# Joint stages between scans: one fixed order of beats, convolution on four engines, gate on GpSimd, input norm folded into in_proj, rows backwards last

## The chip, the core and the metric

The kernel runs on one core of one Trainium2 chip. The metric is the device time of one execution in microseconds (us). The core's engines are named as in the profile: PE (matrix products; PEld loads its weights), DVE (VectorE), ACT (ScalarE), POOL (GpSimd) and SP, whose queue issues the DMAs.

## What is computed

The input is four images of 64 x 64 positions with 96 channels. Two layers of a selective-scan block are followed by two layers of linear attention and a quantised feed-forward net on the 4096 positions of each image as tokens. Layers 0 and 1 are, cut to what matters (`_gn` is a group norm over 32 groups of 3 channels, without weights):

```python
x = x + block(_gn(x))                      # twice, with each layer's weights
# block:
xz = jnp.einsum('bhwc,ec->bhwe', x, in_proj_w)          # 96 -> 384 channels
xp, z = jnp.split(xz, 2, axis=-1)
xc = conv3x3_per_channel(xp) + conv_b                   # 192 channels, 'SAME'
xc = jax.nn.silu(xc)
# four directions: rows, columns, rows backwards, columns backwards
ys = _selective_scan(xs, delta, A, Bmat, Cmat, Dp)      # h = exp(dl*A)*h + dl*u*B; y = C.h + D*u
y = ys[:, 0] + flip(ys[:, 2]) + wh_back(ys[:, 1]) + wh_back(flip(ys[:, 3]))
y = _layernorm(y, out_norm_w, out_norm_b)               # over 192 channels
y = y * jax.nn.silu(z)
return jnp.einsum('bhwd,cd->bhwc', y, out_proj_w)       # 192 -> 96 channels
```

## The kernel before

The four images go in two pairs, and a pair in one layer is a unit of work: layer 0 pair 0, layer 0 pair 1, layer 1 pair 0, layer 1 pair 1. The 2 x 192 inner channels of a pair fill three tiles of 128 partitions, `u0` and `u1` with 128 channels of one image each and `u2` with the last 64 of both. For each unit `hybrid_kernel` (L940) calls `between_scans` (L142) and then the scan, `PairScan.run` (L483). After the fourth scan `token_layers` (L889) does the rest.

A *scan* has 48 steps (4 directions `k` x 4 chunks of 1024 positions x 3 tiles) of 8 groups each. All its instructions on PE, DVE, ACT and POOL keep the order of the program through `InOrder` (L56). The sum over the state is transposed on PE, copied by ACT to the tile `ysum` (L661 to L665) and stored to `y` in device memory; directions after the first load the sum so far (`kept`, L653) and add to it. The directions come in the order 0 to 3, and in directions 2 and 3 the chunks go from the last to the first (`chunk_of`, L385); 1 and 3 run along columns. `begin` (L394) makes the first projections and the first step size (`xps`, `delta`, `du`, `dut`) of a scan and is called from the joint stage before it. Each step multiplies `h` by `cb` on POOL as its last work.

A *joint stage* (`between_scans`) is made of two generators, and the first stage has only the first of them. `scan_inputs` (L157) prepares the unit to come: it loads `wi`, makes nine diagonal matrices `diag` from the convolution weights on POOL (L172), clears the edges of three padded images `img`, and then `project` (L216) takes one image's 512 positions at a time: load x, normalise it on DVE with mean and 1/deviation of the group norm (`xn`, L223), three products on PE (`ips`, L227), two copies by ACT into `img` (L229, L230) and two silus to `zs`, stored to `zg` (L233 to L236). There are 16 such calls. The convolution is cut into pieces of 8 or 16 rows of one tile. `conv_product` (L183) does 8 rows on PE, nine taps as products of the shifted image with `diag` (`cps`, L189; each product appears as two records), then a silu on ACT (L190). `conv_chain` (L194) does 16 rows on DVE: one TENSOR_SCALAR (L203) and eight SCALAR_TENSOR_TENSOR (L205, "a tap" below), then a silu (L206). PE has eight pieces, DVE eight of double length. For layer 0, whose group norm has not been measured by an earlier unit, `measure` (L208) loads each image once more for its statistics, in the first joint stage only.

`scan_outputs` (L272) finishes the unit whose scan has just ended, in 16 groups of 256 positions from the first row on: load `zt`, `xr` and `ys` (L285 to L296), statistics of the layer norm on DVE (`ystats` L303, `ymv` L304, `ln_ve` L79), the power -1/2 on POOL (`ln_rs`, L81), `shift` on DVE (L307), normalise on ACT (L311), transposes on PE (`pt`, L319), four evictions with weight and bias on ACT (`gt`, L321), the gate `gt*zt` on DVE (L328), the out-projection on PE (`po`, L335), the residual sum on DVE (`xo`, L337) with its store, and two statistics for the next layer's group norm (`GroupNorm.take`, L117). At the end two chains of small operations (`GroupNorm.norm`, L120) give the next layer's mean and 1/deviation, one for each image.

Within a joint stage the order of each engine's instructions is decided by a scheduler, which starts from the order in which the generators' pieces are called. The stage's tiles come from pools of its own, whose memory is shared with the scan's pools; in the profile `wo`, the first tile to be loaded, is issued after the last store of `ysum`. PSUM has five buffers for inputs (`mm`), two for `pt` and one for `po`.

The scan's long-lived pool `s_q` holds, with one buffer each, the tiles `delta`, `du`, `dut` and the parts of the projection for even chunks.

Of the kernel before, what the change touches and what calls it, by code (L numbers as in the profile page):

```python
# [18 lines left out]
NB = 4  # L26
# [8 lines left out]
K = 4  # L35
NP = 32 * 3
# [7 lines left out]

# [5 lines left out]

# [4 lines left out]

class InOrder:  # L56

# [5 lines left out]

# [11 lines left out]

# [8 lines left out]

class ScanLayer:

# [21 lines left out]

class GroupNorm:


    def __init__(self, pool, pn, name, parts):
        self.pool, self.pn, self.name, self.n = pool, pn, name, 0
        self.stats = pool.tile([C, parts, 6], F32, name=f"{name}_stats", bufs=1)

    def take(self, nc, v):
        nc.vector.bn_stats(self.stats[:, self.n], v)  # L117
        self.n += 1

    def norm(self, nc, pp, tag, cst, half):  # L120
        pool = self.pool
        mv = pool.tile([C, 2], F32, name="mv")
        nc.vector.bn_aggr(mv, self.stats.rearrange("c g s -> c (g s)"))

        gm = pp.tile([C, 1], F32, name="gm", tag=tag)
        nc.tensor.matmul(gm, cst["group"], mv[:, 0:1], start=True, stop=True)
        mean = pool.tile([C, 1], F32, name="mean")
        nc.vector.tensor_copy(mean, gm)
        dev = pool.tile([C, 1], F32, name="dev")
        nc.vector.tensor_tensor(dev, mv[:, 0:1], mean, ALU.subtract)  # L130
        spread = pool.tile([C, 1], F32, name="spread")
        nc.vector.scalar_tensor_tensor(spread, dev, dev, mv[:, 1:2], ALU.mult, ALU.add)
        gv = pp.tile([C, 1], F32, name="gv", tag=tag)
        nc.tensor.matmul(gv, cst["group"], spread, start=True, stop=True)
        rs = rstd_of(nc, pool, gv, [C, 1], "gn", half[:C, 0:1])
        kept = self.pn.tile([C, 2], F32, name=f"{self.name}_norm")
        nc.vector.tensor_copy(kept[:, 0:1], mean)
        nc.vector.tensor_copy(kept[:, 1:2], rs)
        return kept[:, 0:1], kept[:, 1:2]


def between_scans(tc, cst, ident, half, pn, u, before, scan, after):  # L142


    with ExitStack() as stage:
        ins = scan_inputs(tc, stage, cst, ident, half, pn, u, scan, *after)
        if before is not None:
            pp = stage.enter_context(tc.tile_pool(name="c_ps", bufs=2, space=PSUM))
            outs = scan_outputs(tc, stage, cst, ident, half, pn, *before, pp)
            for g, _ in enumerate(outs):  # L150
                for _ in range(2 if g % 4 == 3 else 1):
                    next(ins, None)
        for _ in ins:
            pass


def scan_inputs(tc, stage, cst, ident, half, pn, u, scan, layer, pr):  # L157

    nc = tc.nc
    par, zg, x_src = layer.par, layer.zg[pr], layer.x_src
    pa = stage.enter_context(tc.tile_pool(name="a", bufs=1))
    p2 = stage.enter_context(tc.tile_pool(name="a2", bufs=3))
    pp = stage.enter_context(tc.tile_pool(name="a_ps", bufs=5, space=PSUM))

    wi = pa.tile([C, 2, 2 * DI], F32, name="wi")
    nc.sync.dma_start(out=wi, in_=layer.w["wi"].rearrange("i c d -> c i d"))

    diag = pa.tile([128, 9, 128], F32, name="diag")  # L170
    for tap in range(9):
        nc.gpsimd.tensor_scalar(diag[:, tap], ident, par[:, 0, P_CONV + tap : P_CONV + tap + 1], None, ALU.mult)  # L172

    imgs = []
    for j in range(3):
        img = pa.tile([128, HW + 2, HW + 2], F32, name=f"img{j}", tag=f"img{j}")
# [4 lines left out]
        imgs.append(img)  # L181

    def conv_product(j, c):  # L183

        ps = pp.tile([128, 8, HW], F32, name="cps", tag="mm")
        for tap in range(9):
            dy, dx = divmod(tap, 3)
            v = imgs[j][:, c + dy : c + dy + 8, dx : dx + HW]
            nc.tensor.matmul(ps, diag[:, tap], v, start=(tap == 0), stop=(tap == 8))  # L189
        nc.scalar.activation(  # L190
            u[j][:, HW * c : HW * (c + 8)], ps.rearrange("p h w -> p (h w)"), AF.Silu, bias=par[:, 0, P_CB : P_CB + 1]
        )

    def conv_chain(j, c):  # L194

        s, cols = j // 2, slice(HW * c, HW * (c + 16))
        to = u[j][:, cols].rearrange("p (h w) -> p h w", w=HW)
        for tap in range(9):
            dy, dx = divmod(tap, 3)
            v = imgs[j][:, c + dy : c + dy + 16, dx : dx + HW]  # L200
            weight = par[:, s, P_CONV + tap : P_CONV + tap + 1]
            if tap == 0:
                nc.vector.tensor_scalar(to, v, weight, par[:, s, P_CB : P_CB + 1], ALU.mult, ALU.add)  # L203
            else:
                nc.vector.scalar_tensor_tensor(to, v, weight, to, ALU.mult, ALU.add)  # L205
        nc.scalar.activation(u[j][:, cols], u[j][:, cols], AF.Silu)  # L206

    def measure(b):  # L208
        norm = GroupNorm(p2, pn, f"gn{b}", 8)
        for g in range(8):  # L210
            xt = p2.tile([C, 512], F32, name="xt", bufs=4)
# [882 lines left out]
```

## Time and profile before

| what | us |
|---|---|
| median of three runs | 10594.62 (10580.44 to 10601.88) |
| span of the profiled execution | 10592.1 |
| joint stage 0 (inputs alone) | 156.4 |
| joint stages 1, 2, 3 (outputs and inputs) | 205.6, 209.1, 202.4 |
| four scans | 2293 to 2298 each |
| token stage, with the last outputs | 635.8 |

The stages can be told apart in the trace by the scan operations on DVE: a joint stage lies between the last TENSOR_TENSOR_SCAN of one unit and the first of the next. The lines of the profile are read as follows. A line of a group has the line of the code, engine, operation, output <- inputs, shapes, and then the busy time in us, the mean duration of one in ns, and the idle time ahead of it with what ended it. A line of a wait has the engine with the waiting line, what it waited for, the total in us, how often and the longest. A line of the timeline has the start and the duration in us.

The whole of the profiled execution keeps DVE busy for 9610.8 us, POOL for 9023.9, ACT for 8761.4 and PE for 8027.2.

### The profile page before, as it was taken

What the parts mean: (1) busy time and instruction counts of PE and PEld (TensorE: products, weight loads), DVE (VectorE), ACT (ScalarE), POOL (GpSimd) and SP (SyncE); (2) the same over time, 40 slices, a digit from 0 to 9 for tenths busy, and PEclk for the clock granted to TensorE, in tenths of its full rate; (3) what the DMA queues carried; (4) which work ended last, traced back from release to release, by engine and by line L of the source; (5) the groups of instructions that cost most, each with busy time, mean ns of one, the idle gap of its engine ahead of it and who ended that gap; (6) DMA issues with size and microseconds to landing.
All of it is one profiled execution on the core that took longest, in us unless ns stands there. A gap on an engine that the chain in (4) does not pass through costs nothing. (4 is left out here: it accounts for less than half of the span.)

```text
span 10592.1 us, 142441 instructions
## 1 busy us (share of the span) xinstructions
PE 8027.2 (76%) x47648; PEld 5946.6 (56%) x47648; DVE 9610.8 (91%) x6922; ACT 8761.4 (83%) x18779; POOL 9023.9 (85%) x5298
## 2 busy tenths in 40 slices
PE   7777777777777777777877777777877777777666
PEld 4555555554555555555555555555555565555554
DVE  8999999998999999998899999999799999999755
ACT  6888888885988888887788888888688888888666
POOL 3999999993999999997599999999399999999645
PEclk9888898989888898998888988898888989899877
DMA  5677777776677777777567777777667777777710
GB/s 155 208 212 216 220 220 218 219 218 164 205 212 212 218 220 218 217 220 210 158 206 213 219 220 220 223 213 216 162 207 212 216 213 225 221 217 213 195 32 25
DMA packets 905174, 2120.41 MB, mean 200 GB/s; under 512 B 330582, under 2 KB 640152, under 8 KB 706712
## 3 DMA queue, kind: packets, MB, share of 16 engines
q1 hardware_dynamic: 904440, 2111.30, 69.5%
q8 instruction: 378, 6.19, 0.3%
q14 instruction: 356, 2.92, 0.1%
HBM read 1949.56 MB, written 161.48 MB: 199 GB/s over the span
## 5 line engine op out<-in xcount | busy, mean ns | idle before, releaser
L71 POOL TENSOR_TENSOR h<-h,cb 128x1024 f32<-128x1024 f32 x3072 | 7196.5, 2367 | 226.4 <-issue 62.6
L71 DVE TENSOR_TENSOR_SCAN h<-da,last,bp 128x1024 f32<-128x1024 f32 x2064 | 4736.6, 2335 | 146.7 <-PE bp L71 22.8
L71 ACT ACTIVATE x<-dut,bt 128x128 f32<-128x128 f32 x12288 | 3495.9, 371 | 1.4 <-PE bp L71 1.1
L71 PE MATMUL yp<-ident,h 128*128 128x128 f32 x24576 | 3359.4, 297 | 10.5 <-POOL h L71 10.5
L71 PEld LDWEIGHTS yp<-ident,h 128*128 128x128 f32 x24576 | 3188.5, 157 | 126.6 <-issue 76.6
L71 ACT ACTIVATE da<-delta,amat 128x1024 f32<-128x1024 f32 x2752 | 3062.3, 1139 | 96.6 <-DVE h L71 95.8
L71 PE MATMUL bp<-ident,x 128*128 128x128 f32 x10240 | 1678.5, 316 | 1294.1 <-DVE h L71 956.8
L71 PEld LDWEIGHTS bp<-ident,x 128*128 128x128 f32 x10240 | 1361.3, 163 | 1854.8 <-ACT x L71 1017.4
L71 DVE TENSOR_TENSOR bp<-du,bp 128x1024 f32<-128x1024 f32 x1472 | 1780.5, 1214 | 259.8 <-PE bp L71 257.8
L71 DVE TENSOR_TENSOR_SCAN h<-da,bp 128x1024 f32<-128x1024 f32 x688 | 1537.7, 2275 | 49.9 <-ACT da L71 9.6
L71 PE MATMUL bp<-bparts,sel 96*128 96x512 bf16 x2944 | 920.5, 398 | 756.3 <-DVE h L71 740.4
L71 PEld LDWEIGHTS <-sel 96*128 96x128 bf16 x2944 | 226.8, 100 | 1550.2 <-DVE h L71 1037.8
L71 ACT ACTIVATE bp<-delta,amat 128x1024 f32<-128x1024 f32 x320 | 358.1, 1119 | 526.3 <-DVE h L71 524.6
L71 POOL TENSOR_TENSOR dbu<-du,bb 128x1024 f32<-128x1024 f32 x320 | 755.7, 2362 | 0.0
L71 DVE TENSOR_TENSOR_SCAN h<-bp,last,dbu 128x1024 f32<-128x1024 f32 x240 | 558.9, 2329 | 16.9 <-POOL dbu L71 15.9
L71 PE MATMUL xps<-u,wx 128*76 128x512 f32 x720 | 532.2, 824 | 0.0
L71 POOL COPY last<-h 128x2 f32<-128x2 f32 x1152 | 217.7, 189 | 357.2 <-DVE h L71 355.5
L81 POOL TENSOR_TENSOR ln_rs<-ln_ve,half 128x4 f32<-128x4 f32 x64 | 89.8, 1403 | 483.1 <-DVE ln_ve L79 405.9
L71 ACT ACT_TABLE_LOAD x380 | 487.5, 1283 | 15.9 <-PE bp L71 9.2
L71 POOL TENSOR_TENSOR du<-delta,u 128x1024 f32<-128x1024 f32 x188 | 496.8, 2642 | 0.0
L71 PE MATMUL dps<-cdt,wdt 12*128 12x512 f32 x752 | 433.6, 656 | 0.0
L71 ACT COPY ysum<-yp 128x1024 f32<-128x1024 f32 x192 | 194.5, 1013 | 287.1 <-PE yp L71 287.1
(159 smaller groups left out, 6312.6 us busy)
## 6 DMA issues: line engine op xcount, KB each, us to landing
cb<-crow SPq DMA_DIRECT2D x1024, 1024.0 KB
cb<-crow SPq DMA_DIRECT2D x1024, 512.0 KB
bb<-crow SPq DMA_DIRECT2D x384, 256.0 KB
bb<-crow SPq DMA_DIRECT2D x128, 512.0 KB
y<-ysum SPq DMA_DIRECT2D x192, 256.0 KB
kept<-y SPq DMA_DIRECT2D x160, 256.0 KB
y<-ysum SPq DMA_DIRECT2D x64, 512.0 KB
zt<-zg SPq DMA_DIRECT2D x64, 384.0 KB
```

The lines of the kernel that those rows point to most:

```text
L71: return self.tc.keep_in_program_order(getattr(self.engine, op)(*args, **kwargs))
L81: nc.gpsimd.tensor_tensor(rs, ve, half, ALU.pow)
```

## The change

The joint stage becomes two classes, `Inputs` and `Outputs`, whose methods are called in one written order of 16 beats and a lead beat of -1. All four compute engines keep that order through `InOrder`; SP's DMAs don't. In beat b POOL gates group b-1; ACT normalises group b; DVE takes the statistics of group b+1, POOL its `ln_rs` and `shift` (two small POOL operations, where it was one on DVE); up to three image pieces are projected; group b is transposed; group b-1 is projected out and stored. Six times in a beat `fill` hands out convolution taps to three kinds of piece: 5 taps a beat to DVE, 3 products to PE, 3 taps to the new third kind, in which ACT multiplies an 8-row image by the tap's weight into one of two `parts` buffers and POOL adds it. DVE has seven pieces of 16 rows and one of 8, PE five of 8, POOL with ACT four of 8. A piece can start when `PIECES` says that its rows have been projected.

The group norm of the input is folded into the in-projection: `fold` multiplies `wi` by 1/deviation (two DVE operations), and six small products give a shift that enters as a bias when ACT evicts the projection. x is no longer normalised. `diag` is built by ACT. One chain of small operations makes the norms of both images. The evictions of the transposes are two a group instead of four. In the token stage the outputs run through the same class, with the gate on DVE.

The scan takes the directions in the order 0, 1, 3, 2, and the outputs go from the last rows to the first. `ysum`, and with it the last store, moves to the pool that outlives the scan; `wi`, the first four pieces of x and `parts` use memory of that pool that is free by then. In the first joint stage the statistics of the second pair come at the end of the order. The diff, cut to its core:

```diff
 K = 4
+ORDER = (0, 1, 3, 2)
...
+class GroupNorms:
...
+        for i in range(2):
+            nc.vector.bn_aggr(mv[:, i], self.stats[:, i].rearrange("c g s -> c (g s)"))
+
+        gm = pp.tile([C, 2], F32, name="gm", tag=tag)
+        nc.tensor.matmul(gm, cst["group"], mv[:, :, 0], start=True, stop=True)
...
+        ve = pool.tile([C, 2], F32, name="gn_ve")
+        nc.vector.tensor_scalar(ve, gv, EPS, None, ALU.add)
+        nc.gpsimd.tensor_tensor(kept[:, 1], ve, half[:C, 0:2], ALU.pow)
+        return [(kept[:, 0, i : i + 1], kept[:, 1, i : i + 1]) for i in range(2)]
...
 def between_scans(tc, cst, ident, half, pn, u, before, scan, after):
+        nc = InOrder(tc)
+        ins = Inputs(nc, tc, stage, cst, ident, half, pn, u, scan.spare, *after)
+        outs = None
         if before is not None:
             pp = stage.enter_context(tc.tile_pool(name="c_ps", bufs=2, space=PSUM))
+            outs = Outputs(nc, tc, stage, cst, ident, half, pn, *before, pp)
+        if not ins.layer.norms[ins.pr]:
+            ins.measure(0)
+        for piece in range(4):
+            ins.load(piece)
+        ins.fold()
+        convs = [Handout(ins.jobs(engine), share) for engine, share in SHARES.items()]
+        beginnings = scan.begin(nc, ins.pp)
+        for beat in range(-LEAD, BEATS + 1):
+            now = outs is not None and 0 <= beat < BEATS
+            past = outs is not None and beat > 0
+            ready = PIECES[beat + LEAD]
+            def fill():
+                if beat < BEATS:
+                    for one in convs:
+                        one.go(ready)
+            if past:
+                outs.gate(beat - 1)
+            fill()
+            if now:
+                outs.normalise(beat)
+            if outs is not None:
+                for g in range(0 if beat == -LEAD else beat + 2, min(beat + 3, BEATS)):
+                    outs.load(g)
+                if 0 <= beat + 1 < BEATS:
+                    outs.measure(beat + 1)
+                    outs.scale(beat + 1)
+            fill()
+            for piece in range(*PIECES[beat + LEAD : beat + LEAD + 2]):
+                if piece + 4 < BEATS:
+                    ins.load(piece + 4)
+                ins.project(piece)
+            fill()
+            if now:
+                outs.turn(beat)
+            fill()
+            if past:
+                outs.project(beat - 1)
+            ready = PIECES[beat + LEAD + 1]
+            fill()
+            if past:
+                outs.store(beat - 1)
+            fill()
+            if beat >= BEGIN:
+                for _ in range(4):
+                    next(beginnings, None)
         for _ in beginnings:
             pass
+        while any([one.go(BEATS) for one in convs]):
+            pass
+        if outs is not None:
+            outs.close()
+        if not ins.layer.norms[1]:
+            ins.measure(1)
+BEATS = NT // 2
+PIECES = (0, 3, 5, 6, 8, 9, 11, 12, 14, 15, 16, 16, 16, 16, 16, 16, 16, 16, 16, 16)
+LEAD = 1
+BEGIN = 8
+CONVS = {'vector': ((0, 0, 16), (2, 0, 16), (0, 16, 16), (2, 16, 16), (0, 32, 16), (2, 32, 16), (2, 48, 16), (0, 48, 8)), 'tensor': ((1, 0, 8), (1, 16, 8), (1, 32, 8), (1, 48, 8), (1, 40, 8)), 'gpsimd': ((1, 8, 8), (1, 24, 8), (1, 56, 8), (0, 56, 8))}
+SHARES = {'vector': 5, 'tensor': 3, 'gpsimd': 3}
+class Handout:
+    def __init__(self, pieces, share):
+        self.pieces, self.share, self.owed = pieces, share, 0.0
+        self.ready = next(pieces, None)
+    def go(self, beat):
+        self.owed = min(self.owed + self.share / 6, self.share)
+        while self.owed >= 1 and self.ready is not None and beat >= self.ready:
+            self.owed -= 1
+            self.ready = next(self.pieces, None)
+        return self.ready is not None
+class Inputs:
...
+        self.parts = spare([128, 2, 8, HW], "parts", "ysum")
+        self.wi = spare([C, 2, 2 * DI], "wi", "dut")
+        self.first = [spare([C, 2, 512], "x01", "delta"), spare([C, 2, 512], "x23", "du")]
...
+    def fold(self):
+        nc, norms = self.nc, self.layer.norms[self.pr]
+        for i, (mean, rstd) in enumerate(norms):
+            nc.vector.tensor_scalar(self.wi[:, i], self.wi[:, i], rstd, None, ALU.mult)
+        ps = self.pp.tile([128, 2, 3], F32, name="shps", tag="mm")
+        for i, (mean, rstd) in enumerate(norms):
+            for q in range(3):
+                v = self.wi[:, i, 128 * q : 128 * q + 128]
+                nc.tensor.matmul(ps[:, i, q : q + 1], v, mean, start=True, stop=True)
+        nc.vector.tensor_scalar(self.shift, ps, -1.0, None, ALU.mult)
+        for j in range(3):
+            self.edges(j)
+        par = self.layer.par
         for tap in range(9):
+            nc.scalar.mul(self.diag[:, tap], self.ident, par[:, 0, P_CONV + tap : P_CONV + tap + 1])
...
-        nc.vector.tensor_scalar(xn, xn, *layer.norms[pr][i], ALU.subtract, ALU.mult)
-        nc.scalar.copy(imgs[i][:, rows, 1 : HW + 1], pss[0])
-        nc.scalar.copy(imgs[2][mine, rows, 1 : HW + 1], pss[1][mine])
+        nc.scalar.activation(self.imgs[i][:, rows, 1 : HW + 1], pss[0], AF.Identity, bias=shift[:, 0:1])
+        nc.scalar.activation(
+            self.imgs[2][mine, rows, 1 : HW + 1], pss[1][mine], AF.Identity, bias=shift[mine, 1:2]
+        )
...
+    def jobs(self, engine):
+        nc, par = self.nc, self.layer.par
+        for j, row, n in CONVS[engine]:
+            s, cols = j // 2, slice(HW * row, HW * (row + n))
+            last = min(HW // 8 - 1, (row + n) // 8)
+            after = 2 * last + (j > 0) + 1
+            to = self.u[j][:, cols].rearrange("p (h w) -> p h w", w=HW)
+            bias = par[:, s, P_CB : P_CB + 1]
+            yield after
+            if engine == "tensor":
+                to = self.pp.tile([128, 8, HW], F32, name="cps", tag="mm")
+            for tap in range(9):
+                dy, dx = divmod(tap, 3)
+                v = self.imgs[j][:, row + dy : row + dy + n, dx : dx + HW]
+                weight = par[:, s, P_CONV + tap : P_CONV + tap + 1]
+                if engine == "tensor":
+                    nc.tensor.matmul(to, self.diag[:, tap], v, start=(tap == 0), stop=(tap == 8))
+                elif engine == "vector" and tap == 0:
+                    nc.vector.tensor_scalar(to, v, weight, bias, ALU.mult, ALU.add)
+                elif engine == "vector":
+                    nc.vector.scalar_tensor_tensor(to, v, weight, to, ALU.mult, ALU.add)
+                elif tap == 0:
+                    nc.scalar.activation(to, v, AF.Identity, scale=weight, bias=bias)
+                else:
+                    part = self.parts[:, tap % 2]
+                    nc.scalar.mul(part, v, weight)
+                    nc.gpsimd.tensor_tensor(to, to, part, ALU.add)
+                yield after
+            if engine == "tensor":
+                nc.scalar.activation(self.u[j][:, cols], to.rearrange("p h w -> p (h w)"), AF.Silu, bias=bias)
+            else:
+                nc.scalar.activation(self.u[j][:, cols], self.u[j][:, cols], AF.Silu)
+class Outputs:
...
+        self.gating = nc.gpsimd if summed == "po" else nc.vector
...
+    def load(self, g):
+        nc, layer, pr, at = self.nc, self.layer, self.pr, L - 256 * (g + 1)
...
+    def scale(self, g):
+        nc, (mv,) = self.nc, self.scaled[g]
+        half = self.half[:, 0:4].rearrange("p (t i) -> p t i", i=2)
+        rs = rstd_of(nc, self.p2, mv[:, :, :, 1], [128, 2, 2], "ln", half)
+        shift = self.p2.tile([128, 2, 2], F32, name="shift")
+        nc.gpsimd.tensor_tensor(shift, mv[:, :, :, 0], rs, ALU.mult)
+        nc.gpsimd.tensor_scalar(shift, shift, -1.0, None, ALU.mult)
+        self.scaled[g] = rs, shift
...
+    def turn(self, g):
+        nc, par, (_, _, ys) = self.nc, self.layer.par, self.loaded[g]
+        self.gated[g] = gt = self.p2.tile([128, 3, 2, 128], F32, name="gt", bufs=2)
+        for s, js, firsts in ((0, slice(0, 2), (0, 256)), (1, slice(2, 3), (128,))):
+            pt = self.pp.tile([128, len(firsts), 2, 128], F32, name="pt", tag=self.turned)
+            for j, first in enumerate(firsts):
+                for t in range(2):
+                    nc.tensor.transpose(pt[:, j, t], ys[:, t, first : first + 128], self.ident)
+            nc.scalar.activation(
+                gt[:, js], pt, AF.Identity, bias=par[:, s, P_NB : P_NB + 1], scale=par[:, s, P_NW : P_NW + 1]
+            )
+    def gate(self, g):
+        gt, (zt, _, _) = self.gated[g], self.loaded[g]
+        self.gating.tensor_tensor(gt, gt, zt.rearrange("p j (t q) -> p j t q", q=128), ALU.mult)
...
 class PairScan:
-    steps = [(k, ci, j) for k in range(K) for ci in range(L // T) for j in range(3)]
+    steps = [(k, ci, j) for k in ORDER for ci in range(L // T) for j in range(3)]
...
-            tile_ = p2.tile([128, T // 128, 128], F32, name="ysum", bufs=1)
+            tile_ = self.pq.tile([128, T // 128, 128], F32, name="ysum", bufs=1)
...
-                    if k + 1 < K:
-                        weights[k + 1] = load_weights(nc, pk, w, k + 1)
+                    for then in ORDER[ORDER.index(k) + 1 :][:1]:
+                        weights[then] = load_weights(nc, pk, w, then)
...
-        outs = scan_outputs(tc, stage, cst, ident, half, None, *outputs, pp, "mm", "o")
+        outs = Outputs(nc, tc, stage, cst, ident, half, None, *outputs, pp, "mm", "o").one_by_one()
```

## The prediction

> **What bounds the kernel now.** I read the page's busy table and slices first, then a table of busy time over the five stretches between scans, then the groups by shape, waits and timeline of one stretch. The four scans take 2293 to 2298 us each, 9183 of the 10592.1 us, and keep their instructions (only the order of their directions changes). So the change is worth what it does in the four joint stages and the token stage:
>
> ```profile
> core 0: us, PE busy (x) PEld busy (x) DVE busy (x) ACT busy (x) POOL busy (x), PEclk, DMA share, GB/s
> 0.00:156.40 156.40, 118.82 (x298) 52.42 (x298) 118.58 (x158) 61.92 (x98) 9.61 (x31) 0.99 0.40 116
> 2449.50:2655.10 205.60, 167.85 (x530) 85.44 (x530) 159.12 (x331) 116.17 (x224) 36.66 (x41) 0.91 0.51 144
> 4949.70:5158.80 209.10, 172.73 (x530) 86.98 (x530) 159.19 (x331) 116.31 (x224) 36.95 (x41) 0.89 0.50 141
> 7457.30:7659.70 202.40, 172.63 (x714) 97.63 (x714) 134.20 (x269) 123.16 (x240) 30.83 (x39) 0.92 0.56 152
> ```
>
> The columns are length, then each engine's busy time. PE is the fullest at 168 to 173 us of 202 to 209, DVE second; GpSimd has 37. The four stages are 773.5 us, the three joint ones with outputs 205.7 on average. Waits of the first of these:
>
> ```profile
> POOL ln_rs L81 <- DVE ln_ve L79: 126.6, 15, 23.9
> ACT ys L311 <- DVE shift L307: 38.5, 9, 14.9
> DVE ystats L303 <- DMA ys<-y: 15.8, 5, 12.9
> PE ips L227 <- DMA zt<-zg: 15.3, 1, 15.3
> ```
>
> GpSimd idles behind DVE, ScalarE waits for DVE's small norm operations, and the head is a wait: the scan before ends at 2449.8, but its last y store is issued at 2454.8 to 2457.5, the stage's first loads follow from 2459.6, the first projection runs at 2469.05, the first tap on DVE at 2480.1.
>
> The groups give prices (last columns: busy us, mean ns):
>
> ```profile
> L205 DVE SCALAR_TENSOR_TENSOR u<-img,par,u 128x1024 f32<-128x1024 f32 x64 | 79.8, 1272 | 0.1
> L189 PE MATMUL cps<-img,diag 128*128 128x512 f32 x144 | 65.6, 596 | 0.0
> L328 DVE TENSOR_TENSOR gt<-gt,zt 128x768 f32<-128x768 f32 x16 | 15.2, 951 | 2.6 <-ACT gt L321 2.6
> ```
>
> **What the skill says.** "SBUF — State Buffer", section "SBUF: two separate sides": a DVE operation with two SBUF inputs (or in a two-port mode) and a GpSimd operation take their shared port pair as "an exclusive lock, not a bandwidth split"; the loser blocks fully. The trace agrees. One small `ln_rs` on GpSimd, beside a bn_stats, then beside taps and a gate:
>
> ```profile
> 2536.13 0.35 DVE L303 BATCH_NORM_STATS2 ystats<-ys 128x6 f32<-128x192 f32 x1
> 2536.39 1.01 POOL L81 TENSOR_TENSOR ln_rs<-ln_ve,half 128x4 f32<-128x4 f32 x1 [13.79 <-DVE ln_ve L79]
> ...
> 2552.89 1.27 DVE L205 SCALAR_TENSOR_TENSOR u<-img,par,u 128x1024 f32<-128x1024 f32 x1
> 2553.14 2.75 POOL L81 TENSOR_TENSOR ln_rs<-ln_ve,half 128x4 f32<-128x4 f32 x1 [4.87 <-DVE ln_ve L79]
> 2554.08 0.94 DVE L328 TENSOR_TENSOR gt<-gt,zt 128x768 f32<-128x768 f32 x1
> ```
>
> 1.01 us free; 2.75 beside a tap and a gate, ending about 1.0 after the tap's port hold and gate are over. This is decisive: the change gives GpSimd work just where DVE runs taps. "GPSIMD Engine Reference", section 3.1 "Elementwise — side-by-side cycle accounting", gives about 2.6 cycles an element; this trace has it as 2.367 us for 128x1024 and 0.674 for 128x256, that is 2.2 ns an element plus 0.1. "ScalarE: Activation LUTs", section "What ACT_TABLE_LOAD costs": each pointer operand adds about 93 ns; here 0.58 without and 0.681 with a bias at 128x512.
>
> **The change, part by part** (one joint stage with outputs; from 2449.8).
> *PE.* 8 convolution pieces of 65.6 / 8 = 8.2 us become 5: −24.6, so 168 → 143.
> *DVE.* Gate −15.2, normalised x −10.5 (0.54 each when not blocked, 16 of them), shift −2.6, half a piece of taps −5.4, one norm chain for two images about −1, two weight scalings +1: 159 → about 126.
> *ScalarE.* Four pieces' multiplies, 36 x 0.68 = +24.5; nine diag tiles +3.3; biases on evictions 64 x 0.09 = +6; two transposed evictions a group in place of four, (2 x 0.563 + 2 x 0.456) − (0.56 + 0.79, the latter worked from the slope) = 0.69 x 16 = −11: 116 → about 139.
> *GpSimd.* 16 gates of 768 elements, 0.1 + 768 x 0.0022 = 1.8 us, 29; 32 adds of 512, 1.24 us, 40; ln_rs 16; two shift operations 0.35 x 16 = 5.6: about 90 where it had 17 outside diag. Diag leaves it.
> *The port.* On it now: taps 86, gates 15, and normalised x 8.5 beside 16 of ln_rs, some 125. After: taps 7 x (0.55 + 8 x 1.196) + 5.6 = 76.5, weight scalings 2, GpSimd 80 to 88 (start-ups may overlap): 158 to 167. That is more than PE's 143: **the bound moves from PE to the port**, and the bn_stats (32 us), aggregates and residual adds on DVE hide beside GpSimd.
> *Head.* wi and four x tiles go to spare slots of the scan's pool and ysum out of the stage's memory, so SP issues these five loads before the last store and not after it. First projection near 2456 (last h*cb ends 2452.4, its copy 2454.6) instead of 2469; first tap near 2473, as it needs five projected pieces, with three pieces of some 3 us a beat. SP has no fixed order: wo, zt, xr and ys still stand behind the last y store, two DMAs instead of four; ys comes about 5 us earlier. From the scan's end to the first tap: 23 us instead of 30.
> *Tail.* After the last gate: out-projection 2.0, xo 0.7, two stats 0.7, aggregates 1.0, one norm chain about 3 instead of two, bp 1.2: 9 us.
> *Order.* Engines are held to the order of beats, so a late operation holds all behind it: behind a late add on GpSimd stand the next gate (then out-projection on PE) and the next ln_rs and shift (then ScalarE's normalise and its queue of evictions). That is new, as the scheduler's order was also fixed but put no work of length on GpSimd. Rows backwards, directions 0,1,3,2: what the last direction wrote last is loaded last, so no y load waits for a store but the first ones; free, since those waits end in the head.
> So the stage is 23 + (158 to 167) + 9 = 190 to 199 with no port idle. I take the low end, 158, with 3% idle, 163: 195, which is −10.7 a stage, **−32 for three**.
> *Stage 0.* No outputs, no gates. All adds are new: port 76.5 + 40 = 117 instead of 93; the first tap needs five pieces and both images' statistics, about 47.5 where it was 38.9. The rest of the statistics, 16 x 0.685 = 11 us, now comes after the taps and not between them, beside the begin of the scan. 47.5 + 117 = 164.5 against 156.4: **+8** (−8, if the adds fit into the gaps between the tap chains, to +14).
> *Token stage.* Gates stay on DVE; ScalarE has 11 us less in the phase of outputs (9982 to 10099), GpSimd two small operations more per group: **−3** (−8 to +5; its end is image work behind the outputs).
> *Scans.* Same work, other order; a direction takes 568 to 580 us already: 0, ±6 each. The y of the last step is stored by two DMAs.
> Sum: −32 + 8 − 3 = −27. The profiled execution has a span of 10592.1, the median of the runs is 10594.6, 2.5 more, so the sum stands on the median: **10567**.
>
> **Rivals.**
> (a) *The port is hidden.* If locks collide seldom, for instance because taps and GpSimd operations interleave between bn_stats and residual adds, beats are bound by PE and ScalarE, 143 and 139: gap 23 + 143 + 9 + 3 of slack = 178, −27 a stage; stage 0 −8, token −3: −92, **10502**. For: a third of DVE's time needs no lock. Against: DVE's lock time plus GpSimd's exceed 158 in any order.
> (b) *Slower: GpSimd starves.* DVE took the port twice running (2.75 us above, longest 3.09 for 1.0 of work), so in a tap chain GpSimd's short operations come through late. With two parts buffers ScalarE's multiply then waits for GpSimd's add, and the queue behind it (evictions for PE) stands, and DVE in turn waits for pieces: the port idles. Price: one tap of 1.2 us lost per beat, 16 beats, is 19 us: gap 195 + 17 to 19 = 212 to 214, +6 to +8 a stage; stage 0 at its +14, token +5: about +40, **10635**. It decides once the idle exceeds 0.7 us a beat: then the gap passes 203 to 204 and stage 0 tips the sum. For: the wait is in the trace. Against: GpSimd's own hold blocks DVE as well, which evens the turns.
> (c) *No net effect*: idle near 0.5 us a beat, 10.5 us a stage over the 190; this lies within the forecast's own range.
>
> **How the numbers follow.** The forecast has 0.50: its own range 10540 to 10612 from gap 190 to 203 and the bounds of stage 0 and the scans; (a) 0.24; (b) 0.26. About 0.2%, 21 us, is what a measurement of this kernel can tell from no change. Of the forecast's half, 0.28 is faster by more, 0.19 within, 0.03 slower; (a) is all faster; (b) 0.04 within, 0.22 slower. Faster 0.52, same 0.23, slower 0.25. To leave out no more than 2 in 10, the range reaches to 10500 and 10632.
>
> **What would show it.** In the after trace: gaps near 195; gate 1.8 us when free and 2.5 to 3.5 beside taps; adds 1.25 free and above 2 beside taps; tap chains stretched from 1.196 us a tap; PE busy near 143. If gates and adds show their free times and the gap is near 178, (a) holds. If DVE waits for ScalarE's evictions and GpSimd's `ln_rs` holds ScalarE's normalise for whole microseconds each beat, (b). A first projection still near 2469 would refute the head; a scan off by more than 6 us, the rest.

## The result and the profile after

The changed kernel took 10572.99 us (median; 10560.81 to 10581.51) against 10594.64 before: ratio 0.9979, 95% interval 0.9972 to 0.9985. The forecast was 10567. Yet the total hides terms that were off in both directions. The profiled execution spans 10571.8 us, 20.3 less than before:

| us | before | after | difference | forecast |
|---|---|---|---|---|
| joint stage 0 (to the first scan operation) | 156.7 | 179.7 | +23.0 | +8 |
| joint stages 1, 2, 3 | 205.6, 209.1, 202.4 | 192.1, 191.7, 186.7 | −46.6 | −32 |
| four scans together | 9182.8 | 9175.4 | −7.4 | 0 (±6 each) |
| token stage | 635.6 | 646.2 | +10.6 | −3 |

The table of busy time by stretch after, with the same columns as before (length, PE, PEld, DVE, ACT, POOL, clock, DMA share, GB/s):

```profile
0.00:179.70 179.70, 107.72 (x249) 47.67 (x249) 140.85 (x131) 93.78 (x147) 64.62 (x52) 0.87 0.33 101
2474.90:2667.20 192.30, 156.75 (x486) 81.79 (x486) 165.01 (x280) 139.73 (x241) 142.70 (x111) 0.87 0.51 150
4962.60:5154.40 191.80, 156.53 (x485) 82.17 (x485) 163.73 (x280) 139.56 (x241) 141.58 (x111) 0.89 0.51 151
7447.50:7634.30 186.80, 159.10 (x672) 93.78 (x672) 150.62 (x225) 144.83 (x255) 138.44 (x110) 0.91 0.53 156
```

In joint stage 1 PE has gone from 168 to 157 us and DVE has *risen* from 159 to 165, although by the forecast's count it lost some 33 us of work. The groups of that stage show why (in-order operations carry the line of their helper, L60; the last columns are busy us, mean ns and idle time ahead):

```profile
L60 DVE SCALAR_TENSOR_TENSOR u<-img,par,u 128x1024 f32<-128x1024 f32 x56 | 86.1, 1537 | 1.4
L60 POOL TENSOR_TENSOR u<-u,parts 128x512 f32<-128x512 f32 x32 | 50.1, 1564 | 13.8 <-ACT parts L60 11.4 <-DMA ys<-y 1.7
L60 POOL TENSOR_TENSOR gt<-gt,zt 128x768 f32<-128x768 f32 x16 | 35.1, 2192 | 8.0 <-ACT gt L60 8.0
L60 POOL TENSOR_TENSOR ln_rs<-ln_ve,half 128x4 f32<-128x4 f32 x16 | 30.2, 1887 | 14.4 <-DVE ln_ve L60 14.1
L60 POOL TENSOR_SCALAR shift<-shift 128x4 f32<-128x4 f32 x16 | 17.7, 1104 | 1.4
L60 DVE TENSOR_SCALAR ln_ve<-ymv 128x4 f32<-128x4 f32 x16 | 12.3, 772 | 0.5
L60 DVE BATCH_NORM_STATS2 ystats<-ys 128x6 f32<-128x192 f32 x64 | 18.4, 342 | 8.7 <-DMA ys<-y 8.6
L60 DVE TENSOR_TENSOR xo<-xr,po 96x512 f32<-96x512 f32 x16 | 10.8, 678 | 9.7 <-PE po L60 9.7
```

Three of DVE's groups in the same stage before:

```profile
L79 DVE TENSOR_SCALAR ln_ve<-ymv 128x4 f32<-128x4 f32 x16 | 2.5, 159 | 0.1
L303 DVE BATCH_NORM_STATS2 ystats<-ys 128x6 f32<-128x192 f32 x64 | 20.3, 343 | 15.9 <-DMA ys<-y 15.8
L337 DVE TENSOR_TENSOR xo<-xr,po 96x512 f32<-96x512 f32 x16 | 10.8, 677 | 3.5 <-PE po L335 3.3
```

A tap takes 1.54 us (1.27 before), an add 1.56 and a gate 2.19 where the shortest take 1.25 and 1.80; `ln_rs` 1.89 for 1.01 of work; a `ln_ve` of 0.16 us takes 0.77 on DVE. Half of the adds and gates run almost free (medians 1.27 and 1.81), but half of the `ln_rs` take 2.0 or more. The bn_stats, at 0.342, is untouched (0.343 before), and so is the residual sum `xo`. The wait for the port is inside the recorded duration of the waiting operation, which is why busy time rose where work fell. From the timeline, around 2560 us:

```profile
2559.40 1.80 POOL L60 TENSOR_TENSOR gt<-gt,zt 128x768 f32<-128x768 f32 x1
2559.66 1.56 DVE L60 TENSOR_SCALAR ln_ve<-ymv 128x4 f32<-128x4 f32 x1
2561.14 6.32 DVE L60 SCALAR_TENSOR_TENSOR u<-img,par,u 128x1024 f32<-128x1024 f32 x4
2561.16 1.25 POOL L60 TENSOR_TENSOR u<-u,parts 128x512 f32<-128x512 f32 x1
2562.38 2.01 POOL L60 TENSOR_TENSOR ln_rs<-ln_ve,half 128x4 f32<-128x4 f32 x1
```

The gate runs free (1.80) and `ln_ve` waits until it is over; then four taps take 6.32 us (4 x 1.196 = 4.8 without waiting), because an add goes first.

A joint stage divides at DVE's first and last tap. In stage 1 the head went from 30.6 to 18.2 us, the stretch of taps *grew* from 143.0 to 164.4, and the rest after the last tap shrank from 32.0 to 9.5: before, taps were done early and PE's convolution and the last outputs were left over. So the gain lies at both ends and the port takes part of it back in the middle.

### The profile page after: what moved, and what is told of

It reads as the page before. It is cut to its first block, busy times and chain, and to the rows that moved or that the text cites. A ratio compares the mean times of both kernels' runs of the same rounds, so it can differ in the third digit from the quotient of the medians.

```text
span 10571.8 us, 142296 instructions
## 1 busy us (share of the span) xinstructions
PE 7963.0 (75%) x47464; PEld 5918.9 (56%) x47464; DVE 9656.2 (91%) x6730; ACT 8848.4 (84%) x18835; POOL 9402.3 (89%) x5562
## 4 chain that ended last, share of the span: by engine, by line
ACT 36%; issue 17%; DVE 17%; PE 16%; POOL 10%; DMA 2%; SPq 0%; DVEq 0%; POOLq 0%; ACTq 0%
ACT x L60 16%; ACT da L60 13%; DVE h L60 9%; POOL h L60 6%; PE yp L60 6%; PE bp L60 5%; DVE bp L60 4%; ACT bp L60 2%; DVE u L60 2%; PE xps L60 1%; POOL dbu L60 1%; DMA cb<-crow 1%; ACT L60 1%; PE dps L60 1%; PE dups L60 1%
## 5 line engine op out<-in xcount | busy, mean ns | idle before, releaser
L60 POOL TENSOR_TENSOR h<-h,cb 128x1024 f32<-128x1024 f32 x3072 | 7194.0, 2366 | 224.4 <-issue 64.2
L60 DVE TENSOR_TENSOR_SCAN h<-da,last,bp 128x1024 f32<-128x1024 f32 x2064 | 4736.5, 2335 | 143.7 <-PE bp L60 20.7
L60 ACT ACTIVATE x<-dut,bt 128x128 f32<-128x128 f32 x12288 | 3495.0, 370 | 0.9 <-PE bp L60 0.7
L60 PE MATMUL yp<-ident,h 128*128 128x128 f32 x24576 | 3350.8, 296 | 10.2 <-POOL h L60 10.2
L60 PEld LDWEIGHTS yp<-ident,h 128*128 128x128 f32 x24576 | 3176.6, 156 | 125.5 <-issue 75.6
L60 ACT ACTIVATE da<-delta,amat 128x1024 f32<-128x1024 f32 x2752 | 3060.1, 1138 | 101.7 <-DVE h L60 96.9
L60 PE MATMUL bp<-ident,x 128*128 128x128 f32 x10240 | 1673.8, 315 | 1301.0 <-DVE h L60 951.7
L60 PEld LDWEIGHTS bp<-ident,x 128*128 128x128 f32 x10240 | 1355.4, 162 | 1863.3 <-ACT x L60 1019.6
L60 DVE TENSOR_TENSOR bp<-du,bp 128x1024 f32<-128x1024 f32 x1472 | 1780.6, 1214 | 259.2 <-PE bp L60 257.5
L60 DVE TENSOR_TENSOR_SCAN h<-da,bp 128x1024 f32<-128x1024 f32 x688 | 1537.8, 2274 | 47.2 <-ACT da L60 4.8
L60 PE MATMUL bp<-bparts,sel 96*128 96x512 bf16 x2944 | 921.9, 399 | 759.1 <-DVE h L60 741.7
L60 PEld LDWEIGHTS <-sel 96*128 96x128 bf16 x2944 | 226.5, 100 | 1554.4 <-DVE h L60 1042.1
L60 ACT ACTIVATE bp<-delta,amat 128x1024 f32<-128x1024 f32 x320 | 358.1, 1119 | 529.9 <-DVE h L60 528.1
L60 POOL TENSOR_TENSOR dbu<-du,bb 128x1024 f32<-128x1024 f32 x320 | 755.1, 2360 | 0.0
L60 DVE TENSOR_TENSOR_SCAN h<-bp,last,dbu 128x1024 f32<-128x1024 f32 x240 | 559.0, 2329 | 13.8 <-POOL dbu L60 11.5
L60 PE MATMUL xps<-u,wx 128*76 128x512 f32 x768 | 555.6, 812 | 0.0
L60 POOL COPY last<-h 128x2 f32<-128x2 f32 x1152 | 216.2, 188 | 332.6 <-DVE h L60 323.7
L60 POOL TENSOR_TENSOR du<-delta,u 128x1024 f32<-128x1024 f32 x188 | 496.6, 2642 | 0.0
L60 PE MATMUL dps<-cdt,wdt 12*128 12x512 f32 x768 | 441.5, 655 | 0.0
L60 ACT COPY ysum<-yp 128x1024 f32<-128x1024 f32 x192 | 194.4, 1012 | 284.9 <-PE yp L60 284.9
L60 ACT COPY dut<-dups 128x512 f32<-128x512 f32 x384 | 220.1, 574 | 237.1 <-PE dups L60 237.1
```

The source lines that it names most:

```text
L60: return self.tc.keep_in_program_order(getattr(self.engine, op)(*args, **kwargs))
```

## The experiments

Each states its gaps in the order of joint stages 1, 2, 3, from one profiled execution; gaps of one form repeat within about 1 us, and the token stage took 642.6 to 646.9 in the changed kernel and the five experiments that leave its code and the written order alone. Totals were taken in three sets, each with its own runs of the kernel before (10596.9, 10599.6, 10592.9), so ratios are compared across sets.

### Statistics of the second pair in the beats

```diff
+        measuring = ins.measuring(1) if outs is None else iter(())
...
+            if beat >= 3:
+                next(measuring, None)
...
-        if not ins.layer.norms[1]:
-            ins.measure(1)
+        for _ in measuring:
+            pass
```

> The changed kernel, but in the first joint stage the 16 statistics of the second pair are taken two a beat from beat 3 on, with x tiles of their own, and their norm follows, instead of all of it at the end of DVE's order. Theory (the end of stage 0 is DVE's queue: taps end at 161.1, the statistics and the norm chain stand between them and the first scan at 179.7, and this is all that the prediction missed there): the statistics need no lock on the port and hide beside GpSimd's adds, the first scan starts at 164 to 172, total 8 to 15 us less, near 10560. Rival (the 11 us of DVE time cost the same wherever they stand): 177 to 181, total within 3 us.

The first scan started at 169.7 instead of 179.7; total 10552.6, ratio 0.9957 (0.9940 to 0.9974). The end of stage 0 on DVE in the changed kernel, and then in this one:

```profile
153.08 8.03 DVE L60 SCALAR_TENSOR_TENSOR u<-img,par,u 128x512 f32<-128x512 f32 x8
161.03 2.46 DVE L60 BATCH_NORM_STATS2 gn_stats<-xt 96x6 f32<-96x512 f32 x4
...
173.86 0.69 DVE L60 BATCH_NORM_STATS2 gn_stats<-xt 96x6 f32<-96x512 f32 x1 [0.26 <-DMA xt<-in_x]
174.47 0.58 DVE L60 BATCH_NORM_AGGREGATE mv<-gn_stats 96x2 f32<-96x48 f32 x2
...
178.39 1.23 DVE L60 TENSOR_TENSOR bp<-du,bp 128x1024 f32<-128x1024 f32 x1 [1.19 <-PE bp L60]
```

```profile
157.82 8.04 DVE L60 SCALAR_TENSOR_TENSOR u<-img,par,u 128x512 f32<-128x512 f32 x8
168.26 1.23 DVE L60 TENSOR_TENSOR bp<-du,bp 128x1024 f32<-128x1024 f32 x1 [2.41 <-PE bp L60]
```

In the changed kernel the statistics and their loads hold the scan's first product for 17 us. Among the taps they push the last tap back by 4.8 us only (161.1 to 165.9): of their 11 us more than half hid. The theory holds for the stage; the total, by its ratio, fell by some 23, but the two intervals overlap.

### Token stage: shift on DVE

```diff
-        nc.gpsimd.tensor_tensor(shift, mv[:, :, :, 0], rs, ALU.mult)
-        nc.gpsimd.tensor_scalar(shift, shift, -1.0, None, ALU.mult)
+        if self.summed == "po":
+            nc.gpsimd.tensor_tensor(shift, mv[:, :, :, 0], rs, ALU.mult)
+            nc.gpsimd.tensor_scalar(shift, shift, -1.0, None, ALU.mult)
+        else:
+            nc.vector.scalar_tensor_tensor(shift, mv[:, :, :, 0], -1.0, rs, ALU.mult, ALU.mult)
```

> The changed kernel, but in the token stage alone shift is one DVE operation again and not two on GpSimd. Theory (the token stage is longer because shift waits on GpSimd behind the token norms' work, up to 5.5 us at a time, and ScalarE's normalise waits for shift): token stage 646 goes to 634 to 638, total about 10 us less. Rival (the length comes from two evictions and two gt buffers in place of four and three, or from the rows' order): 644 to 648, no difference in total.

The token stage took 635.7 us instead of 646.2 (7 to 11 us less than where it was left alone), the value of before; total 10567.4, ratio 0.9971 (0.9960 to 0.9982). What it removes, in the timeline of the changed kernel:

```profile
9966.53 0.20 POOL L379 TENSOR_TENSOR shift<-ymv,ln_rs 128x4 f32<-128x4 f32 x1
9966.69 5.43 POOL L69 TENSOR_TENSOR tn_rs<-tn_ve,half 128x32 f32<-128x32 f32 x1
9972.09 0.23 POOL L380 TENSOR_SCALAR shift<-shift 128x4 f32<-128x4 f32 x1
9972.36 0.98 ACT L388 ACTIVATE ys<-ys,shift,ln_rs 128x192 f32<-128x192 f32 x2 [6.65 <-POOL shift L380]
```

Between the two small operations GpSimd ran a token norm of 5.43 us, and ScalarE stood still for it. The two evictions and the rows' order together cost nothing that shows there.

### Without GpSimd's adds

```diff
-                    nc.gpsimd.tensor_tensor(to, to, part, ALU.add)
```

> The changed kernel with GpSimd's 32 adds per joint stage left out (the four ScalarE/GpSimd convolution pieces then keep only their first tap; ScalarE's multiplies stay). Theory (the shared port is the bound of the beats): 50 us of GpSimd's 143 go, DVE's taps fall from 1.54 us towards 1.27 and the gap from 192, 192, 187 to between 165 and 178, total 60 to 100 us less with stage 0. Rival (the written order with ScalarE and PE, at 140 and 157 us, is the bound): gaps within 3 us of before, total less than 15 us less.

Gaps 172.9, 172.7, 166.6; taps 1.412 us; DVE's busy time in stage 1 from 165.0 to 146.9; the span 10489.1, one time of 10490.9. Inside the theory's interval, far from the rival's. This kernel leaves work out and was timed once. Leaving the adds out also shortens GpSimd's queue and frees `parts` sooner, so the gap alone does not tell the port from the queue; but in stage 1 some 18 of the 19 us are busy time of DVE, whose work is the same. On average 19.5 us for 32 adds is 0.6 us an add, half of its own 1.25: the other half had hidden.

### Gate on DVE

```diff
-        self.gating = nc.gpsimd if summed == "po" else nc.vector
+        self.gating = nc.vector
```

> The changed kernel with the gate of the joint stages on DVE (0.95 us each) in place of GpSimd (1.8 us), 16 a stage, same place in the order. Theory (shared port): both forms hold the port, DVE's for half the time, so the port is relieved of about 14 us and the gaps fall by 4 to 12 us each, total 12 to 36 us less. Rival (DVE's own queue is the bound, GpSimd's work hides): DVE has 15 us more a stage, the gaps rise by 8 to 15, total 24 to 45 us more.

Gaps 193.7, 193.0, 182.9: +1.6, +1.3, −3.8. Total 10569.2, ratio 0.9973 (0.9963 to 0.9984), like the changed kernel. Neither theory had this. DVE's groups in stage 1:

```profile
L60 DVE SCALAR_TENSOR_TENSOR u<-img,par,u 128x1024 f32<-128x1024 f32 x56 | 76.9, 1374 | 1.4
L60 DVE TENSOR_TENSOR gt<-gt,zt 128x768 f32<-128x768 f32 x16 | 15.5, 966 | 3.4 <-ACT gt L60 3.4
L60 DVE TENSOR_SCALAR ln_ve<-ymv 128x4 f32<-128x4 f32 x16 | 4.7, 292 | 0.5
```

Taps are 9.2 us shorter and `ln_ve` 7.6, and the gate takes back 15.5. So the sum of holds on the port is not what ends the stage, since that sum fell by 14 us (16 gates of 1.8 us against 0.95). What fits best is DVE's queue: its own work *and* what it waits for, the port and other engines. DVE's busy time in the stage fell from 165.0 to 160.7 us, and its waits between the first tap and the last took that back: 9.9 us for the out-projection (8.3 in the changed kernel) and a new one, for the eviction ahead of the gate:

```profile
DVE gt L60 <- ACT gt L60: 3.4, 1, 3.4
```

Stage 3, where DVE has no statistics for a next layer, gains; there DVE was busy for 150.6 of 186.8 us in the changed kernel, against 165.0 of 192.3 in stage 1. That this is why it gains was not tested.

### One line of the change in the kernel before

```diff
-            tile_ = p2.tile([128, T // 128, 128], F32, name="ysum", bufs=1)
+            tile_ = self.pq.tile([128, T // 128, 128], F32, name="ysum", bufs=1)
```

> The kernel before with one line of the change: ysum lies in the pool that outlives the scan. Theory (part of the shorter head is that the stage's first loads no longer wait for the last y store): wo is issued at about 5 us after the scan's end instead of 9.8, the first projection moves from 19.3 to 14 to 16 us after the scan's end and the gaps of 205.6, 209.1, 202.4 fall by 3 to 6 us each, total 10 to 20 us less than before. Rival (ys waits for the y store in any case, and the scheduler's order lets nothing else ahead): gaps within 2 us, no difference in total.

In stage 1 the first projection ran at 16.2 us after the scan's end instead of 19.3. Gaps 203.8, 203.7, 198.5 (−1.8, −5.4, −3.9), token stage 629.4 (−6.2), total 10584.6, ratio 0.9987 (0.9980 to 0.9993). `wo` was issued 4.1 us after the scan's end instead of 9.8. The theory holds for stages 2 and 3 and the total; the gap of stage 1 moved no more than the rival allows, though its head is shorter. By the ratios `ysum` alone is worth 0.13% of the whole change's 0.21%, with intervals that leave room on both sides. In the changed kernel the first projection ran at 6.4; the early `wi` and x are what is left to explain the rest, and no run took them alone.

### One piece from GpSimd to PE

```diff
-CONVS = {... 'tensor': ((1, 0, 8), (1, 16, 8), (1, 32, 8), (1, 48, 8), (1, 40, 8)), 'gpsimd': ((1, 8, 8), (1, 24, 8), (1, 56, 8), (0, 56, 8))}
-SHARES = {'vector': 5, 'tensor': 3, 'gpsimd': 3}
+CONVS = {... 'tensor': ((1, 0, 8), (1, 16, 8), (1, 32, 8), (1, 40, 8), (1, 48, 8), (1, 56, 8)), 'gpsimd': ((1, 8, 8), (1, 24, 8), (0, 56, 8))}
+SHARES = {'vector': 5, 'tensor': 3.6, 'gpsimd': 2.4}
```

> The changed kernel with one convolution piece moved from ScalarE and GpSimd to PE (three and six pieces instead of four and five; the shares per beat 2.4 and 3.6). Theory (the port bounds the beats; without all 32 adds a gap fell by 19.5 us): 8 adds less are worth 4 to 9 us a joint stage and 4 to 6 in stage 0, total 15 to 30 us less than the changed kernel, although PE has 8 us more a stage. Rival (PE, at 157 of 192 us, is by now as much of a bound as the port): gaps within 2 us or longer, total unchanged or up to 15 more.

Gaps 178.5, 179.0, 181.7 (−13.6, −12.7, −5.0), stage 0 6.5 us shorter, total 10536.3, ratio 0.9939 (0.9925 to 0.9952): more than forecast. ScalarE's multiplies of the piece go too, and PE's last two pieces change places. The wait tables of DVE alone, from about the first tap to the last of stage 1, in the changed kernel and in this one, have what the lock does not explain:

```profile
DVE xo L60 <- PE po L60: 8.3, 4, 4.0
```

```profile
DVE xo L60 <- PE po L60: 2.3, 4, 0.9
```

DVE's busy time fell by 8.3 us (165.0 to 156.7) and its wait for the out-projection by 6.0, together about the 13.6. That is 1.7 us for each of the 8 adds, more than an add's own 1.25, so the 0.6 of the run without adds is no fixed price. By the order of the queues that second wait comes through GpSimd: the gate, and `ln_rs` and `shift` ahead of the normalise, stand behind the adds. That would be rival (b)'s mechanism at a smaller price than it was given; no run took that wait away alone, nor ScalarE's multiplies.

### The three edits together

The diffs of the statistics, of the token stage's shift and of the piece, in one kernel.

> The changed kernel with the three edits together: statistics of the second pair in the beats, shift of the token stage on DVE, one convolution piece from GpSimd to PE. Theory: they act in different stages and add up, 10 + 10.5 + 15 to 30, so 10573 goes to 10520 to 10538. Rival (the piece moved to PE gives nothing or costs): 10552 to 10565.

10516.8 us, ratio 0.9922 (0.9910 to 0.9935): faster than both kernels. First scan at 164.9, gaps 178.8, 178.6, 181.4, token stage 634.5. The edits add up.

### Left to the scheduler

```diff
-        nc = InOrder(tc)
+        nc = tc.nc
```

> The changed kernel with the joint stage's engines left to the scheduler instead of held to the written order (same operations, same places of the work). Theory (the sum of work on the port decides, the order only keeps the pair of DVE and GpSimd from idling): gaps of 188 to 202. Rival (the written order is what the gain rests on, the scheduler lets in-projection or outputs run ahead and leaves convolution for the end, as in the kernel before, whose tail after the last tap is 32 us): gaps of 205 or more, total at or above the kernel before.

Gaps 196.8, 196.9, 202.7, token stage 652.9; total 10608.9, ratio 1.0010 (1.0002 to 1.0019), slower than before. By gap stages 1 and 2 go to the theory, stage 3 lies between the two claims, by total the rival is right. The three joint stages still took 20.7 us less than before, of the 46.6 that the written order gives; stage 0 (180.5) and the token stage take that back, so without the written order the change as a whole gains nothing. In stage 3 the last tap came at 151.9 us and DVE then waited for what was left, 31.2 us of it at once:

```profile
DVE bp L60 <- PE bp L60: 31.2, 1, 31.2
```

Why the token stage, whose code is the same, took 6.7 us more (6.0 above the longest where it was left alone) is open.

### Old order of the directions

```diff
-ORDER = (0, 1, 3, 2)
+ORDER = (0, 1, 2, 3)
```

> The changed kernel with the directions in the order 0, 1, 2, 3 again; the outputs still go from the last rows to the first. Theory (ys needs the last columns-backwards store, four DMAs instead of two and touching every row): the first ys load is issued 2 to 3 us later, DVE's first statistics, which stand ahead of the first tap in its order, are 2 to 4 us later, and with them the gap; total 6 to 12 us more. Rival (free, the wait ends in the head beside the first projections): gaps within 1 us; the scans between 2289 and 2299 as in all runs.

The first ys load came 1.9 us later, gaps 194.5, 193.4, 188.6 (+2.4, +1.7, +1.9); total 10570.1, ratio 0.9981 (0.9973 to 0.9988), not told apart from 0.9979. The delay is there in the gap, at the low edge of the theory, and too small for the total. The first tap came 1.7, 1.4 and 1.3 us later after the scan's end, so the ys loads are on the path through the head. The scans came to 9169.7 us together, so their −7.4 is not the order of the directions; all runs here lie between 9169.7 and 9187.7, and its cause is open.

### A second piece to PE

```diff
-CONVS = {... 'tensor': (... (1, 48, 8), (1, 56, 8)), 'gpsimd': ((1, 8, 8), (1, 24, 8), (0, 56, 8))}
-SHARES = {'vector': 5, 'tensor': 3.6, 'gpsimd': 2.4}
+CONVS = {... 'tensor': (... (1, 48, 8), (1, 56, 8), (0, 56, 8)), 'gpsimd': ((1, 8, 8), (1, 24, 8))}
+SHARES = {'vector': 5, 'tensor': 4.2, 'gpsimd': 1.8}
```

> The best version so far (statistics in the beats, token shift on DVE, one piece moved to PE) with a second piece moved from GpSimd to PE: two and seven. Theory (port until PE is full): eight adds less are worth up to 13 us as before, but PE's products in the window between first and last tap go from 133 to 141 of 150, so the gap of joint stages 1 and 2 falls by 2 to 7 us, that of stage 3, whose end PE already sets (its last convolution product ends after the last tap by 10 us), rises by 2 to 6; total 0 to 12 us less. Rival (PE is the bound everywhere by now): all gaps rise by 4 to 8, total 15 to 25 more.

Stage 0 161.2 (−3.7 against the version with three edits), gaps 180.1, 180.6, 178.8 (+1.3, +2.0, −2.6), total 10516.2, ratio 0.9930 (0.9917 to 0.9944). No gain, and the signs of the stages are the opposite of what was expected. The optimum is flat here. In stage 1 DVE's busy time fell from 156.6 to 153.3 us, but between the first tap and the last its wait for the out-projection rose from 2.1 to 6.3; what held the out-projection was not settled.

### Shift on DVE in the joint stages

```diff
-        if self.summed == "po":
-            nc.gpsimd.tensor_tensor(shift, mv[:, :, :, 0], rs, ALU.mult)
-            nc.gpsimd.tensor_scalar(shift, shift, -1.0, None, ALU.mult)
-        else:
-            nc.vector.scalar_tensor_tensor(shift, mv[:, :, :, 0], -1.0, rs, ALU.mult, ALU.mult)
-        self.scaled[g] = rs, shift
+        self.scaled[g] = mv, rs, shift
...
     def normalise(self, g):
-        (_, _, ys), (rs, shift) = self.loaded[g], self.scaled.pop(g)
+        (_, _, ys), (mv, rs, shift) = self.loaded[g], self.scaled.pop(g)
+        self.nc.vector.scalar_tensor_tensor(shift, mv[:, :, :, 0], -1.0, rs, ALU.mult, ALU.mult)
```

> The best version so far with shift in the joint stages on DVE too (one operation of 0.16 us, placed in DVE's order just ahead of ScalarE's normalise, a beat after ln_rs) in place of two on GpSimd, which took 24 us a stage with their waits. Theory (a small GpSimd operation costs its wait for a tap, not its own time; DVE does the same unhindered): GpSimd's busy time falls by about 20 us, gaps fall by 2 to 8 us, total 6 to 24 us less. Rival (DVE's queue is the bound, GpSimd's waits cost nothing beyond its own holds): gaps within 1.5 us, or longer by DVE's 2.6 us.

GpSimd's busy time did fall (129.9 to 105.7 us in stage 1), but the gaps went from 178.8, 178.6, 181.4 to 192.9, 192.4, 182.7; total 10555.6, ratio 0.9964 (0.9951 to 0.9976). The first theory fell: DVE does not do `shift` unhindered. The rival's bound, DVE's queue, fits, but not its 2.6 us. DVE's group and two waits of stage 1:

```profile
L60 DVE SCALAR_TENSOR_TENSOR shift<-ymv,ln_rs 128x4 f32<-128x4 f32 x16 | 11.0, 686 | 1.1 <-POOL ln_rs L60 1.1
PEld pt L60 <- ACT ys L60: 29.8, 32, 4.6
ACT ys L60 <- DVE shift L60: 26.8, 11, 4.6
```

A `shift` takes 0.69 us on DVE, where it took 0.16 before, so it waits for the port too. DVE's busy time in stage 1 rose from 156.6 to 165.3 us, 8.7 of the 14.1 by which the gap grew. The rest is waiting: on DVE `shift` stands behind taps that wait for the port, ScalarE waits 26.8 us for it (1.3 in the changed kernel, for GpSimd's shift), PE waits behind ScalarE, and DVE's wait for the out-projection, between the first tap and the last, rose from 2.1 to 6.3. How the two share the 14 us was not separated. On GpSimd `shift` follows its `ln_rs` at once. So giving it to GpSimd was right in the joint stages and wrong in the token stage, for the same reason: what stands ahead of it in the queue.

## Why the prediction was right, and where it was not

*The bound moves to the port.* Right in mechanism as far as PE no longer bounds the stage and DVE and GpSimd wait for each other: rival (a), 178 a gap with free times, is refuted by the durations and by the run without adds. The stretch from first to last tap was put at 163 (158 with 3% idle) and measured 164.4, 163.3, 158.0. As a law the sum of holds failed: the gate on DVE cut it by 14 us and the gaps hardly moved. DVE's queue with its waits for the port fits the runs best, but with one piece less on GpSimd, and with `shift` on DVE, a part of the change goes through waits for other engines, and no run separates the two. PE was put at 143 us and measured 156.7: the convolution lost 20.3 of the 24.6, and the records of the out-projection grew by 4.9. In the rivals, idle of 0.7 and 0.5 us a beat was turned into gaps of 203 and 200.5; over 16 beats it adds 11 and 8 us to the 190, so that both thresholds stand too high.

*Head and tail.* 23 us to the first tap measured 18.1 to 18.4; 9 us after the last tap measured 9.5 to 10.4. The head is nearly the whole way from −32 to −46.6: 14.3 us in three stages. The first projection came as forecast, 6.4 us after the scan's end in stage 1. But the first tap did not wait for five projected pieces: in stage 1 it ran from 2493.18, before PE projected the fifth piece at 2494.10, directly behind the second group's statistics, and these had waited for ys. So the waits for ys, which were called free, set the head, as the old order of the directions confirms: 1.9 us on the first load, 1.7 to 2.4 on the gaps.

*Stage 0, +8.* This step failed. Its taps ended at 161.1, near the 164.5 worked out, but "beside the begin of the scan" was taken as cover for the 11 us of statistics, and DVE is the engine that begins the scan. The sum had no term at all for the way from the last tap to the scan; even without the statistics it is 3.8 us. With x tiles that arrive behind their buffers, and the norm chain, they cost 17 us from tap to product; moved among the taps, 10.0 came back.

*Token stage, −3.* Failed in sign. ScalarE's busy time did fall, from 394.3 to 386.4 us, but not on the path; "two small operations more" were counted by their own time (0.20 and 0.23 us) and not by what GpSimd does between them, one operation of 5.4 us at a time. Putting shift back on DVE gave back the 10.5.

*Rival (b)* did not set the total, yet DVE's wait for the out-projection is there and fell from 8.3 to 2.3 us when a piece left GpSimd. That GpSimd would starve is not what the trace shows: half of its adds took 1.27 us or less.

*The total* came near the forecast by luck: misses of +15 in stage 0 and +14 in the token stage met −15 in the joint stages and −7 in the scans, and the last of these has no known cause.

## What to carry to other kernels

GpSimd is not a free fourth engine beside a DVE that works from SBUF: ahead of handing it work, add up both queues with the lock. No fixed price of a hold came out here: the gates moved from GpSimd to DVE changed next to nothing in two stages, 32 adds cost 0.6 us each on average, and 8 of them, with ScalarE's multiplies, 1.7. In a written order the last things on an engine's queue can be on the path, however small: ask which engine starts the next stage and what stands ahead of that start. A small operation costs what stands ahead of it on the engine to which it is moved; `shift` on GpSimd instead of DVE was worth 14 us in joint stages 1 and 2 and cost 10 in the token stage.

## What the runs showed of the hardware

A TENSOR_SCALAR of 128x4 on DVE, with one SBUF input, waits for GpSimd's hold as a tap does (0.159 us before, 0.772 after; 0.181 without the adds), while bn_stats (0.343 and 0.342) and the residual sum with its PSUM operand (0.677 and 0.678) don't. A GpSimd power of 128x32 took 5.43 us, one of 128x4 1.01. The granted clock of PE was 0.87 in joint stage 1 of the changed kernel and 0.94 with one more piece on PE; it doesn't explain the gap, since the run with shift on DVE had 192.9 us at 0.92.
